# Units of the first conditioner in another order, and its shared expert in halves of 64 array columns

## The chip, the cores and the metric

The kernel runs on one core of a Trainium2 chip. A core has a matrix engine (PE, which loads weights as a separate step, PEld), a vector engine (DVE), a scalar engine for activations (ACT), a general engine (POOL), a sequencer for data movement (SP), and 16 DMA engines. Each engine runs its own instruction list; semaphores order them. The metric is the device time of one execution in microseconds (us), as the median of several runs.

## The reference

The input is x (32 batches of 128 positions of 128 numbers) and a condition vector for each batch. There are two layers. Each adds to x what a gated network computes from a conditioned x. In the first layer the conditioner is a small mixture of experts, and only it is touched here:

```python
topk_w, topk_i = jax.lax.top_k(gate_scores, 2)          # 2 of 4 experts for each batch
w_be = jnp.sum(topk_w[..., None] * onehot, axis=1)      # after normalising topk_w
for e in range(4):
    y = gelu(context_c @ ew1[e] + eb1[e]) @ ew2[e] + eb2[e]
    out = out + w_be[:, e][:, None, None] * mask[e][None, :, None] * y
shared = gelu(context_c @ sw1 + sb1) @ sw2 + sb2
return out + shared
```

The hidden width is 512. The mask drops 42 of the 128 positions for two of the experts. Then follow the first layer's gated network with 8 experts, computed densely, the second conditioner and the second feed-forward part.

## The kernel before, in words

Features lie on the 128 partitions. The 32 batches form 8 blocks of 4 batches, so a block is 128 partitions by 512 columns. All matrix products are in 32-bit floats; the profile shows each as two instructions.

The first conditioner has two kinds of work. The **shared expert** runs on all 8 blocks: `shared_up` (L255) makes four products of 512 columns into `us` (L260), each followed by an activation (L261); `shared_down` (L267) adds four products into `ys` (L271). Blocks 0 to 4 come first, blocks 5 to 7 (from `FIRST` on) after the routed units.

The **routed experts** run only for the chosen batches. Which expert gets which batch is known only on the chip: `schedule` (L331) ranks the batches of each expert and lays two batches of the same expert together as a pair. Thirty-two batches with two experts each give 64 slots. An expert with an odd number of batches leaves one batch over; it becomes a lone unit. There are at least 30 pairs (`LEAST`), pairs 30 and 31 may be missing, and so may each of the four lone units, numbered 32 to 35. For each unit:

- `fetch` (L434) loads the expert's weights (514.5 KB) on SP's queue, five units ahead (`NW` = 6 buffers). The expert's row is read from memory into SP's registers, four pairs at a time.
- `gather` (L451) copies the slots' inputs next to each other on DVE, two units ahead (`AHEAD`). The places are read into DVE's registers, four slots at a time.
- `unit_up` (L485) makes four products into `u` (L497) and four activations (L500); `unit_down` (L506) adds four products into `y` (L513) and DVE adds the gated result into `c0all` (L516, L520).

The width of a unit also depends on the data. `sized` (L468) tests a register on PE, ACT and DVE: the first arm (L472) is for pairs of unmasked experts (two times 128 columns), the other for masked ones (two times 86). For pair 30 and 31 the second arm holds one more test (L478), and each lone unit has its own (L482). In this run's data, by the operations counted in the trace, 16 pairs are 256 wide, 14 are 172 wide, two lone units are 128 and two 86 wide, and pairs 30 and 31 are missing.

`pipelined` (L200) writes the order: up of the next unit, then down of the present one. A planner in the language layer then orders each engine's instructions from this order and from modelled costs, so the traced order can differ: through most of the units here, a down step stands two units behind the up step. A conditional block stays whole. Small pieces of other work (gates, schedule, logits, transposes, folded weights) are put between the shared expert's products by the table `between` (L614).

`by_columns` (L231) makes one product as several, each with its own group of array columns: for n = 64, two products of 64 columns. The gated network uses it already (L236 for `g` and `u`), and its down products (L729) are also of 64 columns.

Of the kernel before, what the change touches and what calls it, by code (L numbers as in the profile page):

```python
# [39 lines left out]
P = 128  # L40
B, S, D = 32, 128, 128
# [7 lines left out]
NC = H // P  # L49
E0, EF, E1 = 4, 8, 8  # L50
# [5 lines left out]
NO_HEAD = (NHEAD, S)  # L56
# [9 lines left out]
NPAIR = B  # L66
LEAST = NPAIR - E0 // 2
# [32 lines left out]
def adaln_ffn(  # L100
# [3 lines left out]
    nc = tc.nc  # L104
# [9 lines left out]
    def mm_tile(name):  # L114
        return psum.tile([P, TB], F32, tag="mm", name=name, bufs=6)

    def y_tile(name):
        return psum.tile([P, TB], F32, tag="y", name=name, bufs=2)

    def const(shape, name, dtype=F32):  # L120
        return cpool.tile(shape, dtype, tag=name, name=name)
# [5 lines left out]
    sw1_t = wpool.tile([P, H], F32, tag="sw1", name="sw1_t")  # L127
    sw2_t = wpool.tile([P, NC, D], F32, tag="sw2", name="sw2_t")
# [7 lines left out]
    xT = [xall[:, b * TB : (b + 1) * TB] for b in range(NB)]  # L136
# [19 lines left out]
    for to, w in zip(downs_t, (s_w2, r_w2[: E1 // 2], r_w2[E1 // 2 :])):  # L156
        n = w.shape[0]
        nc.sync.dma_start(out=to.rearrange("p (e f) -> p e f", e=n), in_=w.rearrange("e d f -> d e f"))

    def col(name, i=0, n=1):  # L160
        return par[:, AT[name].start + i : AT[name].start + i + n]
# [53 lines left out]
    def sums(blk):  # L215
        xb = batches(xT[blk])
        at = slice(blk * BB, (blk + 1) * BB)
        lo = 0
        for to, n in ((head, NHEAD), (prop, NPROP), (wrist, NHEAD)):
            V.tensor_reduce(to[:, at], xb[:, :, lo : lo + n], AX.X, ALU.add)  # L220
            lo += n
# [5 lines left out]
    def before(*point):  # L227
        for do in between.pop(point, ()):
            do()

    def by_columns(ps, w, x, n):  # L231


        for at in range(0, P, n):
            own = slice(at, at + n)
            nc.tensor.matmul(ps[own, :], lhsT=w[:, own], rhs=x, start=True, stop=True)  # L236

# [13 lines left out]
    FIRST = NB - 3  # L253

    def shared_up(blk):  # L255
        h = work.tile([P, NC, TB], F32, tag="h", name=f"hs0_{blk}", bufs=3)
        ps = [mm_tile(f"us_{blk}_{c}") for c in range(NC)]
        for c in range(NC):
            before("up", "s", blk, c)
            nc.tensor.matmul(ps[c], lhsT=sw1_t[:, c * P : (c + 1) * P], rhs=xT[blk], start=True, stop=True)  # L260
            nc.scalar.activation(h[:, c, :], ps[c], AF.Gelu_apprx_tanh, bias=col("sb1", c))  # L261
        if blk < 2:
            for b in range(4 * blk, 4 * blk + 4):
                sums(b)
        return h

    def shared_down(blk, h):  # L267
        y = y_tile(f"ys_{blk}")
        for c in range(NC):
            before("down", "s", blk, c)  # L270
            nc.tensor.matmul(y, lhsT=sw2_t[:, c, :], rhs=h[:, c, :], start=(c == 0), stop=(c == NC - 1))  # L271
        if blk >= FIRST:
            V.scalar_tensor_tensor(c0T[blk], y, col("sb2"), c0T[blk], ALU.add, ALU.add)
        else:
            V.tensor_scalar(c0T[blk], y, col("sb2"), None, ALU.add)
# [49 lines left out]
    batch_at = const([1, NSLOT], "batch_at", I32)  # L325
    expert_at = const([1, NPAIR], "expert_at", I32)
# [65 lines left out]
    def spread_slots():  # L392
        ps = mm_tile("slots_ps")
        n = slot_sums.shape[-1]
        nc.tensor.matmul(ps[:, :n], lhsT=ones, rhs=slot_sums, start=True, stop=True)
        V.tensor_copy(batch_at, ps[:1, NSLOT : 2 * NSLOT])
        V.tensor_copy(expert_at, ps[:1, 2 * NSLOT : 2 * NSLOT + NPAIR])

        V.tensor_scalar(numbers, ps[:1, 2 * NSLOT + NPAIR : n], 1.0 / B, None, ALU.mult)
        V.tensor_copy(gate_of, ps[:, :NSLOT])  # L400
        E = mybir.EngineType
        engines = (E.PE, E.Activation, E.DVE)
        batch["full"], batch["pairs"], *batch["alone"] = registers(numbers, 0, engines, NPAIR, 2 + E0)
        for q in range(NW - 1):
            fetch(q)
        for q in range(AHEAD):
            gather(q)

    tl = const([P, B, E1], "tl")
# [13 lines left out]
    def registers(of, i, engines, top, n=4):  # L423
        return nc.values_load_multi_w_load_instructions(
            of[:, i : i + n], engines=engines, min_val=0, max_val=top,
            skip_runtime_bounds_check_because="sums of 0/1 times constants, within bounds by construction",
        )[1]

    weights, slots, batch = {}, {}, {}


    NUNIT = NPAIR + E0

    def fetch(q):  # L434


        i = q % NW
        if i < 4:
            w = wpool.tile([P, NPCOLS], F32, tag=f"w{i}", name=f"w_{q}")
        else:  # L440
            w = work.tile([P, NPCOLS], F32, tag="bsum", name=f"w_{q}", bufs=2)
        if q < NPAIR:
            if q % 4 == 0:
                batch["e"] = registers(expert_at, q, [mybir.EngineType.SP], (E0 - 1) * P)
            of = bass.ds(batch["e"][q % 4], P)
        else:
            of = slice((q - NPAIR) * P, (q - NPAIR + 1) * P)
        nc.sync.dma_start(out=w, in_=experts[of, :])
        weights[q] = w

    def gather(q):  # L451

        first = 2 * q if q < NPAIR else NPAIR + q
        if first % 4 == 0:
            batch["at"] = registers(batch_at, first, [mybir.EngineType.DVE], (B - 1) * S + NO_HEAD[0])
        batch[q] = batch["at"][first % 4 :][: slots_of(q)]
        x = work.tile([P, 2, S], F32, tag="bc", name=f"x_{q}", bufs=4)
        for i, at in enumerate(batch[q]):
            V.tensor_copy(x[:, i, :], xall[:, bass.ds(at, S)])
        slots[q] = x  # L460

    def slots_of(q):
        return 2 if q < NPAIR else 1

    NW = 6
    AHEAD = 2

    def sized(q, step):  # L468


        if q < NPAIR:
            with tc.If(batch["full"] > q) as cond:  # L472
                step(2, S)
            with cond.Else():
                if q < LEAST:
                    step(2, NSEEN)
                else:
                    with tc.If(batch["pairs"] > q):  # L478
                        step(2, NSEEN)
        else:  # L480
            e = q - NPAIR
            with tc.If(batch["alone"][e] > 0):  # L482
                step(1, S if e < NFULL else NSEEN)

    def unit_up(q):  # L485
        if q + NW - 1 < NUNIT:
            fetch(q + NW - 1)
        if q + AHEAD < NUNIT:
            gather(q + AHEAD)
        w, x = weights[q], slots.pop(q)  # L490
        h = work.tile([P, NC, 2, S], F32, tag="h", name=f"h0_{q}", bufs=3)
        ps = [mm_tile(f"u_{q}_{c}")[:, : 2 * S].rearrange("p (s t) -> p s t", s=2) for c in range(NC)]

        def step(m, n):
            for c in range(NC):
                w1 = w[:, ATP["w1"]][:, c * P : (c + 1) * P]
                nc.tensor.matmul(ps[c][:, :m, :n], lhsT=w1, rhs=x[:, :m, :n], start=True, stop=True)  # L497
            for c in range(NC):
                bias = w[:, ATP["eb1"]][:, c : c + 1]
                nc.scalar.activation(h[:, c, :m, :n], ps[c][:, :m, :n], AF.Gelu_apprx_tanh, bias=bias)  # L500

        sized(q, step)
        return h
# [122 lines left out]
    nc.gpsimd.memset(c0all[:, FIRST * TB :], 0.0)  # L626
    nc.gpsimd.memset(xall[:, NB * TB :], 0.0)
    L0 = {"s": (shared_up, shared_down), "p": (unit_up, unit_down)}
    units = [("s", b) for b in range(FIRST)] + [("p", q) for q in range(NUNIT)]
    units += [("s", b) for b in range(FIRST, NB)]  # L630
    pipelined(units, lambda k, i: L0[k][0](i), lambda k, i, h: L0[k][1](i, h))

# [213 lines left out]
    def sh_up(sb, k):  # L846
        e, c = divmod(k, 2)
        h = work.tile([P, SB, TB], F32, tag="h", name=f"hs_{sb}_{k}", bufs=3)
        for j in range(SB):
            x = x1T[SB * sb + j]  # L850
            g, u = mm_tile(f"g1_{sb}_{k}_{j}"), mm_tile(f"u1_{sb}_{k}_{j}")
            by_columns(g, sws_t[0][:, e, c, :], x, 32)
            by_columns(u, sws_t[1][:, e, c, :], x, 32)
            glu(g, u, h[:, j, :], f"s1_{sb}_{k}_{j}")
        return h
# [61 lines left out]
    units = [("s", sb, k) for sb in range(NS) for k in range(4)]  # L917
# [26 lines left out]
    def unit_down(kind, *at):  # L944
        STAGES[kind][1](*at)

    pipelined(units, unit_up, unit_down, after)
    low_out(1)

# [78 lines left out]
```

## Time and profile before

| what | value |
|---|---|
| median of 3 runs | 978.38 us (978.09 to 978.49) |
| profiled execution | 979.06 us, span 977.3 us |
| granted PE clock | 0.998 |
| PE busy | 962.9 us (99%) |
| DVE, ACT, POOL busy | 630.5, 345.0, 142.2 us |
| shared blocks 0 to 4, with gates and schedule | 4.9 to 46.4 us |
| routed units | 42.1 to 142.8 us |
| shared blocks 5 to 7, with logits and gates | 142.8 to 167.9 us |
| gated network and the rest | 167.9 us to the end |

In the profile, a row names the line, engine and operation, the output and inputs by the program's names, the shape, and how many. `128*64` before a shape means 128 array rows and 64 columns. Rows in order of time give the start, then the length of the merged group. A matmul's record ends with a modelled tail, so groups overlap on paper; the distance between two starts is the time that the first really takes. A bracket tells how long the engine stood idle before, and who is thought to have ended it.

### The profile page before, as it was taken

The page shows a single profiled execution, that of the slowest core. Times are in us where ns is not written, and L with a number is a line of the kernel's source. Part 1 is how long each engine was busy: PE and PEld are TensorE (multiplying, and loading weights), DVE is VectorE, ACT ScalarE, POOL GpSimd, SP SyncE. Part 2 cuts the span into 40 slices and gives each one's busy share as a digit, 9 for nine tenths or more (in the row PEclk, how much of TensorE's full clock was granted, in tenths as well). Part 3 has the DMA queues.
Part 4 walks back from the last instruction along what each step waited for, and adds up shares of the span by engine and source line. Part 5 has one row for each costly group of instructions (what it writes and reads, how often), then busy time and mean ns, then how long its engine had stood idle before and what let it go on. Part 6 is the DMA issues. An engine that isn't in the chain of part 4 may idle for free.

```text
span 977.3 us, 15574 instructions
## 1 busy us (share of the span) xinstructions
PE 962.9 (99%) x5998; PEld 450.8 (46%) x5998; DVE 630.5 (65%) x1130; ACT 345.0 (35%) x615; POOL 142.2 (15%) x151
## 2 busy tenths in 40 slices
PE   7999999999999999999999999999999999999997
PEld 3588974444444444444444444444444443323342
DVE  3444565666866776686676786567667656648593
ACT  5455544223322322232232332222223224335764
POOL 1000001100101011110101011010100001009680
PEclk9999999999999999999999999999999999999999
DMA  9745650000000000000000000000000000000002
GB/s 319 234 132 153 211 182 26 2 1 4 2 1 1 1 1 1 1 2 1 1 2 1 1 2 3 1 1 1 1 1 2 1 3 2 1 7 1 2 1 87
DMA packets 19043, 34.05 MB, mean 35 GB/s; under 512 B 1729, under 2 KB 9921, under 8 KB 18945
## 3 DMA queue, kind: packets, MB, share of 16 engines
q1 hardware_dynamic: 18096, 31.43, 10.3%
q10 hardware_dynamic: 864, 1.52, 0.4%
q8 instruction: 52, 0.85, 0.4%
q14 instruction: 31, 0.25, 0.1%
HBM read 30.59 MB, written 2.36 MB: 34 GB/s over the span
## 4 chain that ended last, share of the span: by engine, by line
PE 84%; DVE 2%; DVEq 0%; issue 0%
PE u L236 25%; PE g L236 25%; PE ya L729 10%; PE yb L729 8%; PE ur L236 6%; PE p_ps L844 2%; PE ul L895 1%; PE us L260 1%; PE ys L271 1%; PE q_ps L844 1%; PE y L513 0%; PE u L497 0%; DVE hf L704 0%; PE fold_ps L247 0%; DVE t L705 0%; DVE t L706 0%
## 5 line engine op out<-in xcount | busy, mean ns | idle before, releaser
L642 ACT ACTIVATE sf<-g 128x512 f32<-128x512 f32 x256 | 152.7, 597 | 438.1 <-PE g L236 432.0
L643 DVE TENSOR_TENSOR hf<-sf,u 128x512 f32<-128x512 f32 x256 | 174.9, 686 | 185.7 <-PE u L236 184.7
L236 PE MATMUL g<-c0all,wg_t 128*64 128x512 f32 x1024 | 270.3, 593 | 0.0
L236 PE MATMUL u<-cg,wu_t 128*64 128x512 f32 x1024 | 270.1, 592 | 0.0
L637 POOL PARTITION_BROADCAST fg<-fgT x64 | 71.9, 1135 | 662.4 <-DVE cg L685 499.1
L236 PEld LDWEIGHTS u<-cg,wu_t 128*64 128x64 f32 x1024 | 75.7, 137 | 145.2 <-issue 124.4
L236 PEld LDWEIGHTS g<-c0all,wg_t 128*64 128x64 f32 x1024 | 75.7, 137 | 120.2 <-issue 108.2
L729 PE MATMUL ya<-t,wd_t 128*64 128x256 f32 x512 | 121.6, 379 | 0.1
L637 POOL PARTITION_BROADCAST rg<-grows x64 | 67.8, 1187 | 145.4 <-DVE hr L878 76.8
L878 DVE TENSOR_TENSOR hr<-ar,rg 128x512 f32<-128x512 f32 x64 | 60.7, 996 | 15.8 <-ACT ar L877 15.8
L729 PEld LDWEIGHTS ya<-t,wd_t 128*64 128x64 f32 x512 | 69.9, 137 | 0.7 <-DVE t L706 0.6
L500 ACT ACTIVATE h<-u,w 128x256 f32<-128x256 f32 (+3 forms) x136 | 50.3, 429 | 54.3 <-PE u L497 54.3
L729 PE MATMUL yb<-hf,a_sum 128*64 128x256 f32 x512 | 69.1, 379 | 0.0
L729 PE MATMUL ya<-t,a_sum 128*64 128x256 f32 x256 | 65.9, 379 | 0.0
L729 PE MATMUL ya<-hf,wd_t 128*64 128x256 f32 x256 | 65.8, 379 | 0.0
L704 DVE TENSOR_TENSOR hf<-hf 128x512 f32<-128x512 f32 x64 | 62.7, 979 | 2.1
L236 PE MATMUL ur<-xall,rw_t 128*32 128x512 f32 x512 | 58.4, 592 | 0.0
L729 PEld LDWEIGHTS ya<-hf,wd_t 128*64 128x64 f32 x256 | 34.9, 137 | 42.8 <-issue 31.9
L513 PE MATMUL y<-h,w 128*128 128x256 f32 (+3 forms) x272 | 53.1, 338 | 1.0 <-DVE t L516 1.0
L497 PE MATMUL u<-x,w 128*128 128x256 f32 (+3 forms) x272 | 53.0, 338 | 1.1 <-DVEq L478 1.1
L497 PEld LDWEIGHTS u<-x,w 128*128 128x128 f32 x272 | 45.3, 190 | 5.7 <-ACT h L500 1.3
L877 ACT ACTIVATE ar<-ur 128x512 f32<-128x512 f32 x64 | 37.9, 598 | 27.6 <-PE ur L236 27.3
(215 smaller groups left out, 961.4 us busy)
## 6 DMA issues: line engine op xcount, KB each, us to landing
w<-in_experts SPq DMA_DIRECT2D x36, 514.5 KB
xall<-in_x SPq DMA_DIRECT2D x8, 256.0 KB
wg_t<-in_w_gate SPq DMA_DIRECT2D x8, 256.0 KB
wu_t<-in_w_up SPq DMA_DIRECT2D x8, 256.0 KB
wd_t<-in_w_down SPq DMA_DIRECT2D x8, 256.0 KB
out<-fin SPq DMA_DIRECT2D x4, 256.0 KB
out<-fin ACTq DMA_DIRECT2D x4, 256.0 KB
downs<-in_r_w SPq DMA_DIRECT2D x2, 256.0 KB
```

The costliest lines, as they stand in the source:

```text
L236: nc.tensor.matmul(ps[own, :], lhsT=w[:, own], rhs=x, start=True, stop=True)
L497: nc.tensor.matmul(ps[c][:, :m, :n], lhsT=w1, rhs=x[:, :m, :n], start=True, stop=True)
L500: nc.scalar.activation(h[:, c, :m, :n], ps[c][:, :m, :n], AF.Gelu_apprx_tanh, bias=bias)
L513: nc.tensor.matmul(y[:, :m, :n], lhsT=w2, rhs=h[:, c, :m, :n], start=(c == 0), stop=(c == NC - 1))
L637: nc.gpsimd.partition_broadcast(bc, row)
L642: nc.scalar.activation(s, ps_gate, AF.Silu)
L643: V.tensor_tensor(h, s, ps_up, ALU.mult)
L704: V.tensor_tensor(b12, b12, b11, ALU.subtract)
L729: nc.tensor.matmul(y[half, n], lhsT=w[:, c, :], rhs=h[:, c, :], start=False, stop=(e == EF - 1 and last))
L844: nc.tensor.matmul(y[32 * j : 32 * (j + 1), :], lhsT=w, rhs=h[:, j, :], start=first, stop=last)
L877: nc.scalar.activation(a, ps, AF.Gelu)
L878: V.tensor_tensor(h[:, j, :], a, gate, ALU.mult)
```

## The change

Two parts. First, the units: a list `UNITS` holds pairs 0 to 29 in order, with the six units that may be missing (30 to 35) put in at even distances: 0-3, 30, 4-7, 31, 8-11, 32, 12-16, 33, 17-20, 34, 21-24, 35, 25-29. `fetch` now takes a place in this list; `gather` still takes a unit's number. SP's registers are still read for four pairs at a time for pairs below 30, and singly for pairs 30 and 31. DVE's registers are read for each unit by itself.

Second, the shared expert: the products at L260 and L271 go through `by_columns` with 64 columns, which now also takes the flags for the first and last product of a sum.

```diff
-    def by_columns(ps, w, x, n):
+    def by_columns(ps, w, x, n, first=True, last=True):
         for at in range(0, P, n):
             own = slice(at, at + n)
-            nc.tensor.matmul(ps[own, :], lhsT=w[:, own], rhs=x, start=True, stop=True)
+            nc.tensor.matmul(ps[own, :], lhsT=w[:, own], rhs=x, start=first, stop=last)
...
-            nc.tensor.matmul(ps[c], lhsT=sw1_t[:, c * P : (c + 1) * P], rhs=xT[blk], start=True, stop=True)
+            by_columns(ps[c], sw1_t[:, c * P : (c + 1) * P], xT[blk], D // 2)
...
-            nc.tensor.matmul(y, lhsT=sw2_t[:, c, :], rhs=h[:, c, :], start=(c == 0), stop=(c == NC - 1))
+            by_columns(y, sw2_t[:, c, :], h[:, c, :], D // 2, c == 0, c == NC - 1)
...
-        for q in range(NW - 1):
-            fetch(q)
-        for q in range(AHEAD):
+        for i in range(NW - 1):
+            fetch(i)
+        for q in UNITS[:AHEAD]:
             gather(q)
...
-    NUNIT = NPAIR + E0
+    UNITS = list(range(LEAST))
+    maybe = list(range(LEAST, NPAIR + E0))
+    for i in reversed(range(len(maybe))):
+        UNITS.insert((i + 1) * LEAST // (len(maybe) + 1), maybe[i])

-    def fetch(q):
-        i = q % NW
+    def fetch(i):
+        q = UNITS[i]
+        i %= NW
...
         if q < NPAIR:
-            if q % 4 == 0:
-                batch["e"] = registers(expert_at, q, [mybir.EngineType.SP], (E0 - 1) * P)
-            of = bass.ds(batch["e"][q % 4], P)
+            def found(n):
+                return registers(expert_at, q, [mybir.EngineType.SP], (E0 - 1) * P, n)
+            if q < LEAST and q % 4 == 0:
+                batch["e"] = found(min(4, LEAST - q))
+            of = bass.ds(batch["e"][q % 4] if q < LEAST else found(1)[0], P)
...
-        if first % 4 == 0:
-            batch["at"] = registers(batch_at, first, [mybir.EngineType.DVE], (B - 1) * S + NO_HEAD[0])
-        batch[q] = batch["at"][first % 4 :][: slots_of(q)]
+        batch[q] = registers(
+            batch_at, first, [mybir.EngineType.DVE], (B - 1) * S + NO_HEAD[0], slots_of(q)
+        )
...
     def unit_up(q):
-        if q + NW - 1 < NUNIT:
-            fetch(q + NW - 1)
-        if q + AHEAD < NUNIT:
-            gather(q + AHEAD)
+        i = UNITS.index(q)
+        if i + NW - 1 < len(UNITS):
+            fetch(i + NW - 1)
+        for ahead in UNITS[i + AHEAD : i + AHEAD + 1]:
+            gather(ahead)
...
-    units = [("s", b) for b in range(FIRST)] + [("p", q) for q in range(NUNIT)]
+    units = [("s", b) for b in range(FIRST)] + [("p", q) for q in UNITS]
```

## The prediction

> **What bounds the kernel now.** I read the page's busy times and its chain first, then the matrix engine (PE) in order of time over the last expert units of the first conditioner, then the branches there, then two places where PE changes its array form.
>
> ```profile
> PE 962.9 (99%) x5998; PEld 450.8 (46%) x5998; DVE 630.5 (65%) x1130; ACT 345.0 (35%) x615; POOL 142.2 (15%) x151
> PE 84%; DVE 2%; DVEq 0%; issue 0%
> ```
>
> PE sets the end: a change counts only by the PE stream time that it adds or the PE gaps that it opens or closes. The edited stage ends where L236 begins, at 167.94 us.
>
> PE in order of time (start, length with the modelled tail, operation, count); starts are subtracted below:
>
> ```profile
> 127.92 1.33 PE L497 MATMUL u<-x,w 128*128 128x172 f32 x8
> 129.08 1.33 PE L513 MATMUL y<-h,w 128*128 128x172 f32 x8
> 130.87 1.43 PE L513 MATMUL y<-h,w 128*128 128x172 f32 x8 [0.46 <-DVE t L516]
> 132.87 1.41 PE L513 MATMUL y<-h,w 128*128 128x172 f32 x8 [0.57 <-DVE t L516]
> 134.12 1.05 PE L497 MATMUL u<-x,w 128*128 128x128 f32 x8
> 136.26 1.13 PE L497 MATMUL u<-x,w 128*128 128x128 f32 x8 [1.10 <-DVEq L478]
> 137.23 1.95 PE L513 MATMUL y<-h,w 128*128 128x128 f32 x16
> 139.02 1.02 PE L497 MATMUL u<-x,w 128*128 128x86 f32 x8
> ...
> 142.78 1.06 PE L260 MATMUL us<-xall,sw_t 128*128 128x512 f32 x2
> ```
>
> A step of a 172-wide pair takes 129.08 - 127.92 = 1.16 us. After it stand gaps: 130.87 - 129.08 - 1.16 = 0.63; 132.87 - 130.87 - 1.16 = 0.84; 136.26 - 134.12 - 0.89 = 1.25. (0.89 is a step of a lone expert, half of 139.02 - 137.23; its eight instructions start 112 ns apart for 128 columns and for 86, so weight loads pace it.) Who ended them is named as DVE, but the branch row says more:
>
> ```profile
> L478 PEldq COMPARE_BRANCH  x4: 202/205/212, 128.0 to 135.6; - x4
> L478 PEldq EVENT_SEMAPHORE  x4: 51/51/51, 130.5 to 135.9; - x4
> ```
>
> Four times PE came to L478, the test for a pair that may be missing, and skipped the body: pairs 30 and 31 are missing here, up and down, and the four lone experts are all present (rows of 128 and 86 columns). A skip makes PE wait for its own last matmul (130.41 by its modelled end), bump its semaphore (130.45) and take another branch; the next load starts at 130.87. The stretch 129.08 to 142.78 is 13.70 us; its work is 3 x 1.16 + 8 x 0.89 = 10.6. Of the 3.1 us left, 0.63 + 0.84 + 1.25 = 2.7 stand at the four skips, the rest is restarts and short waits of lone units.
>
> **Part one, the moved units.** The order becomes 0-3, 30, 4-7, 31, 8-11, 32, 12-16, 33, 17-20, 34, 21-24, 35, 25-29. It moves the skips; it removes none. Each still drains PE, whoever stands next. One skip costs 0.63 to 0.84 by the rows (the two behind 134.12 share 1.25). What differs is the neighbour: pairs 30 and 31 now stand among the 16 pairs that take the first arm of L472, whose branch on PE is short where it is not taken:
>
> ```profile
> L472 PEldq COMPARE_BRANCH  x96: 65/176/340, 36.5 to 135.4; - x96
> ```
>
> 65 ns in place of some 205 takes 0.14 off. So 4 x (0.58 to 0.72), I take 4 x 0.65 = 2.6 against 2.7, and with no gain from the neighbour 4 x 0.74 = 2.9. The lone units' other waits, 3.1 - 2.7 = 0.4, of which about 0.1 belongs to restarts after skips: among pairs of 1.16 to 1.73 us a step nothing waits on their short ScalarE and VectorE steps. Part one: -0.1 - 0.3 = **-0.4 us** (from -0.8 to +0.1).
>
> What moves with the units. The fetches stay 36 of 514.5 KB on SP's queue; the two missing units' weights now pass ahead of pairs 4 and 8. Pair 4's goes out sixth instead of fifth, about 0.9 us later on SP (a register load and a DMA issue more), and lands up to 514.5 KB / 183 GB/s = 2.8 us later (that rate: the 10 us from 40 us on). Six times 514.5 KB at that rate and the 208 GB/s of 30 to 40 us are in by about 51 us, counted from SP's first fetch at 34.8; pair 4 is used at 56.75. Cover gone: up to 2.8 us. Two more SP register loads of 0.30 us stand before fetches that wait 1.8 us for a buffer anyway. On DVE, slot numbers are read for each unit, not for two: some 19 more register loads of 0.34 us and 0.08 after. Where such a load stands before the copies today (124.76 us), DVE still waits 0.66 us for PE's y; over the 172-wide pairs:
>
> ```profile
> 104.00:129.00 25.00, 25.00 (x174) 25.00 (x173) 14.46 (x55) 13.50 (x43) 0.00 (x0) 1.00 0.74 230
> ```
>
> PE is busy 25.00 of 25.00 us here, DVE 14.46, so the loads cost nothing; uncovered they would be 19 x 0.42 = 8 us at most, and nothing in the trace makes DVE that late. Behind a DVE load stand only its own copies for a unit two steps ahead. Weight traffic is at 0.74 of the DMA engines; a lone unit lasts 1.79 us, which asks 514.5 / 1.79 = 287 GB/s for that moment, below the 348 that the stretch from 10 to 20 us shows, with five units fetched ahead.
>
> **Part two, the halves.** PE after that stage, and a place in the gated network where one 128-column transpose stands between 64-column work:
>
> ```profile
> 160.98 7.03 PE L271 MATMUL ys<-hs,sw_t 128*128 128x512 f32 x16
> 167.94 1.08 PE L236 MATMUL g<-c0all,wg_t 128*64 128x512 f32 x4
> 168.85 1.03 PE L236 MATMUL u<-cg,wu_t 128*64 128x512 f32 x4
> ...
> 236.74 0.59 PE L729 MATMUL yb<-hf,wd_t 128*64 128x256 f32 x2
> 237.27 0.33 PE L558 MATMUL fg_ps<-ident,cwT 128*128 128x128 f32 x1
> 237.53 1.08 PE L236 MATMUL g<-c0all,wg_t 128*64 128x512 f32 x4
> 238.43 1.03 PE L236 MATMUL u<-cg,wu_t 128*64 128x512 f32 x4
> ```
>
> A product of 128 columns is two instructions at 0.429, 0.858 us. In halves it is four, two running side by side, and g and u also start 0.86 apart (L236 in steady flow). So 64 products become 128 pairs of halves at no stream time; the 128 further matmuls and loads hide under the streams as L236's do.
>
> What it adds is changes of array form. ys to g: 7.03 is 6.96 by starts, against 16 x 0.429 = 6.866, +0.09; g 0.91 against 0.86, +0.05; so 128 to 64 is **0.145**. The lone transpose: 237.27 - 236.74 = 0.53 against 2 x 0.216, +0.10; 0.26 against 0.11 for the same transpose among 128-column work (160.87 to 160.98), +0.15; g +0.05: a round trip is **0.30**, so 64 to 128 is 0.155. Now count:
> - start: shared block 3 to pair 0, to shared block 4, to pair 1 (42.09, 43.81, 46.39 today): 0.155 + 0.145 + 0.155 = +0.455
> - last pair to shared block 5: +0.145, less 0.04 that its first interval loses today: +0.10
> - round trips for the transposes L544 and L558: +0.60; for L247, 0.30 less 0.085 that ys already loses after it (155.63 to 157.44 is 1.80, four intervals are 1.716): +0.22
> - ys to g is now 64 to 64: -0.145
> - five returns from 32-column or 32-row work (gate, order, slots, times, logits): today +0.105 (149.06 to 150.88 is 1.82 against 1.716), to 64 columns +0.05: -0.27
>
> Sum **+0.96 us**. A rule speaks for more: the Trainium skill, "TensorEngine Tiling (Array Packing)", Tiling Modes, says that changing the tiling mode drains the engine. A full drain would show the tail past the stream (an L236 matmul lasts 0.592, its stream 0.429: 0.163) and then a 64-column load (0.137), 0.30 a change. The list has nine more changes net: 2.7 us. The two rows show half of that, so I take the rows and keep 2.7 as the upper end; the lower is 0.5, if the planner groups work of one form.
>
> **Sum.** +0.96 - 0.4 = +0.55. The profiled execution took 979.06 (span 977.3 and 1.76 around it): 979.6 for one like it. It lay 0.7 above the median of the runs, 978.38, so the median goes to **978.9 us**, +0.06%. The bound for a change that this kernel's measurement can tell is 0.2%, 1.96 us.
>
> **Rivals.**
> - *The planner mixes forms at the seam* (slower). The last units are now real pairs with 1.16 us steps beside shared blocks 5 and 6, and the written order alternates them. If single 64-column products are dealt between the 128-column steps there and about pair 0, each round trip is +0.30. It passes 0.2% from 1.4 / 0.30, five more round trips; six give 978.9 + 1.8 = 980.7, which is also what the drain rule gives. For it: g, u and ya are already dealt singly in the gated network. Against: today the stage keeps shared blocks whole (42.09 to 46.39).
> - *A skip in mid-stream costs more than in the tail* (slower). PE jumps over two bodies and finds the code behind them not there, or the weights of pair 4 late: 2.8 us, 981.7. Against: 96 branches at L472 with 340 ns at most, and the 6 us of cover above.
> - *The scattering hides the skips too* (faster). All 3.1 us go in place of 0.4: 978.38 - 3.1 + 0.96 = 976.2. For it: the gaps are put down to other engines in the PE rows. Against: the wait is PE's on itself, and no neighbour's work can run in it.
> - *The halves change nothing*: switches are free for these shapes, only part one stays: 978.0. Against: both rows above.
>
> **How the numbers follow.** Near-cancelling, 977.9 to 979.9: 0.57. Mixed forms or full drains: 0.17, a third of it below the bound. Mid-stream stall: 0.09. Skips hidden: 0.07. Halves free: 0.10. So faster 0.07, same 0.57 + 0.10 + 0.06 = 0.73, slower 0.20. Leaving out the skips hidden below and the far end above gives 977.0 to 981.2.
>
> **What would show it.** Skips: four L478 semaphore waits on PE, now between about 55 and 85 us, each with a gap of 0.5 to 0.8; none from 129 us on. Halves: L260 and L271 no longer as 128x512 at 128 columns; product starts 0.86 apart; the rows that follow a 128-column step longer by 0.05, those before it by 0.1. The gated network should start 0.3 to 0.8 us later than 167.94 and the rest keep its length. Wrong it would be if PE waits for weights or for x between 55 and 130 us, if the gap at a skip is over 1 us, or if the planner's order of the later stages shifts, whose last 20 us have PE gaps that I haven't counted.

## The result, and the profile after

| | before | changed |
|---|---|---|
| median of 6 runs each | 978.16 us (977.59 to 978.49) | 983.76 us (982.80 to 984.05) |
| ratio | | 1.0052, 95% interval 1.0040 to 1.0064 |
| profiled execution | 979.06 us, span 977.3 | 983.98 us, span 982.2 |
| granted PE clock in it | 0.998 | 0.998 |

The change costs 5.6 us by the medians, 3.9 to 6.3 by the interval. The prediction was 978.9 with a range to 981.2, so it was wrong. In the changed kernel the up and down products of the units are L506 and L522, the shared expert's products are all L236, the test for a missing pair is L486, and L529, L544, L247 and L558 have become L538, L553, L247 and L567.

The page's busy times and chain, changed kernel:

```profile
PE 968.4 (99%) x6126; PEld 444.1 (45%) x6126; DVE 631.3 (64%) x1130; ACT 344.4 (35%) x615; POOL 142.0 (14%) x151
PE 90%; DVE 2%; issue 0%; DVEq 0%
```

PE still sets the end, and it is busy 5.5 us longer. So nearly all of the time went into PE's own stream, not into waits for another engine. PE in order of time, changed kernel, where the shared expert meets the first pairs (`x2` is one half: a 32-bit product shows as two instructions):

```profile
36.95 3.65 PE L236 MATMUL ys<-hs,sw_t 128*64 128x512 f32 x14
40.53 1.99 PE L506 MATMUL u<-x,w 128*128 128x256 f32 x8
42.45 2.80 PE L236 MATMUL ys<-hs,sw_t 128*64 128x512 f32 x12
45.18 1.99 PE L506 MATMUL u<-x,w 128*128 128x256 f32 x8
47.10 1.07 PE L236 MATMUL ys<-hs,sw_t 128*64 128x512 f32 x2
48.10 1.99 PE L522 MATMUL y<-h,w 128*128 128x256 f32 x8
49.94 1.89 PE L506 MATMUL u<-x,w 128*128 128x256 f32 x8
```

The planner treats a half as an instruction like any other. It laid seven halves ahead of pair 0, six between pair 0 and pair 1, and **one alone** behind pair 1. Block 4's eight halves are split here into one (among the seven ahead of pair 0), six and one; the profile does not tell which half is which. Halves of different products can run side by side too, as a `ys` half and a `g` half do below. A half alone does not run in half the time of its product: from 47.10 to 48.10 is 1.00 us, which is the 0.86 of a whole product and 0.14 for changes of form on both sides. Two halves side by side take 0.86 together. So each run with an odd number of halves costs 0.43 more, and there are two here (7 and 1).

The same view of the seam between the last pairs and shared block 5, and what follows:

```profile
140.24 1.07 PE L236 MATMUL us<-xall,sw_t 128*64 128x512 f32 x2
141.25 1.43 PE L522 MATMUL y<-h,w 128*128 128x172 f32 x8
142.61 1.94 PE L236 MATMUL us<-xall,sw_t 128*64 128x512 f32 x8
144.48 1.43 PE L522 MATMUL y<-h,w 128*128 128x172 f32 x8
...
153.15 0.66 PE L553 MATMUL lg_b<-ident,lgT 128*128 128x128 f32 x4
153.74 1.07 PE L236 MATMUL ys<-hs,sw_t 128*64 128x512 f32 x2
154.74 2.87 PE L247 MATMUL fold_ps<-par,downs 128*128 128x32 f32 x24
157.53 3.17 PE L236 MATMUL ys<-hs,sw_t 128*64 128x512 f32 x8
160.48 4.12 PE L236 MATMUL us<-xall,sw_t 128*64 128x512 f32 x16
164.43 1.02 PE L236 MATMUL ys<-hs,sw_t 128*64 128x512 f32 x2
165.38 0.33 PE L567 MATMUL fg_ps<-ident,cwT 128*128 128x128 f32 x1
165.64 6.65 PE L236 MATMUL ys<-hs,sw_t 128*64 128x512 f32 x29
171.71 0.59 PE L236 MATMUL g<-c0all,wg_t 128*64 128x512 f32 x1
172.13 0.59 PE L236 MATMUL ys<-hs,sw_t 128*64 128x512 f32 x1
...
174.18 1.08 PE L236 MATMUL u<-cg,wu_t 128*64 128x512 f32 x4 [0.17 <-DVE cg L694]
```

Halves are dealt between the 172-wide steps (1.36 us each here, 1.17 among their like), one stands between transposes and folding products, and the runs between changes are odd four times: 1 at 140.24, 1 at 153.74, 13 from 157.53 on, and the 15 `ys` halves from 165.64 on. The last of these 15 shares its time with a half of `g` (171.71 and 172.13), which has the same form, so PE's own stream loses nothing there. But the first `u` waits, by way of DVE, for the last `ys`: from its second instruction at 172.13 to `u` are 2.05 us here, and 2.09 in the moved order alone. So the 0.43 by which that `ys` is late counts there too. The row at 157.53 shows something else: its four halves take 2.95 to the next row's start at 160.48, and 1.77 in other profiles of the same kernel. Its cause is in the clock. Windows of 5 us of the same profile, with PE's busy time first and the granted clock third from the end:

```profile
155.00:160.00 5.00, 5.00 (x32) 3.33 (x33) 1.09 (x4) 0.67 (x2) 0.00 (x0) 0.81 0.00 0
160.00:165.00 5.00, 5.00 (x20) 1.47 (x16) 3.23 (x9) 2.87 (x4) 0.00 (x0) 0.85 0.00 0
```

PE is busy throughout, but for 3.41 us from 158.10 on it was given half its clock, which cost 1.7 us.

To sum the parts for all kernels I cut each trace at three starts: the first `ys` product, unit 2's first `u` product, and the first gated unit's last four `yb` products (184.75 us before). The differences of these starts, in us:

| kernel | first product to first ys | ys to unit 2 | unit 2 to last yb | placed by the middle two, against before | ratio to before (95%), from the timed runs |
|---|---|---|---|---|---|
| before | 9.77 | 35.17 | 134.91 | | |
| changed, first profile | 8.48 | 36.73 | 139.76 | +6.41, of it 1.7 the clock | 1.0052 (1.0040 to 1.0064) |
| changed, three more profiles | 9.40, 9.61, 9.37 | 36.73 | 137.96, 138.08, 137.96 | +4.6 to +4.7 | 1.0058 (1.0044 to 1.0071), five runs beside the first of the three |
| moved order alone | 8.80 | 35.17 | 134.75 | -0.16 | 1.0000 (0.9992 to 1.0008) |
| halves alone | 9.50 | 36.73 | 135.70 | +2.35 | 1.0039 (1.0026 to 1.0053) |
| block 4 down whole | 8.54 | 35.19 | 138.05 | +3.16 | 1.0033 (1.0021 to 1.0045) |
| folding products moved | 9.19 | 36.73 | 138.41 | +5.06 | 1.0053 (1.0039 to 1.0066) |
| halves kept together | 9.39 | 35.19 | 135.67 | +0.78 | 1.0009 (1.0001 to 1.0017) |
| halves in blocks 0 to 2 | 9.34 | 35.28 | 134.79 | -0.01 | 1.0000 (0.9991 to 1.0008) |
| missing pairs left out | 9.56 | 35.17 | 132.12 | -2.78 | 0.9973 (0.9964 to 0.9983) |
| one block per pair | 8.43 | 35.17 | 134.24 | -0.67 | 0.9995 (0.9988 to 1.0001) |
| one block for both pairs | 9.66 | 35.17 | 133.67 | -1.24 | 0.9986 (0.9980 to 0.9993) |

From the last `yb` to the kernel's last four products (`o_ps`) it is 785.5 to 785.6 us in every one of them. The first column differs from execution to execution with the start of the clock, not with the change (last section). The changed kernel's cost is thus 1.56 at the start and 3.05 to 3.17 behind it, 4.6 to 4.7 us, which lies in both of its intervals. The medians stand 5.6 and 5.9 us above. A stretch at half clock in some executions is a part of what lies between (below), and the first column may be another; the rest is not placed. For the halves alone the placed 2.35 us is just under its interval (2.5 to 5.2 us).

### The profile page after: what moved, and what is told of

It reads as the page before. It is cut to its first block, busy times and chain, and to the rows that moved or that the text cites. A ratio compares the mean times of both kernels' runs of the same rounds, so it can differ in the third digit from the quotient of the medians.

```text
span 982.2 us, 15841 instructions
## 1 busy us (share of the span) xinstructions
PE 968.4 (99%) x6126; PEld 444.1 (45%) x6126; DVE 631.3 (64%) x1130; ACT 344.4 (35%) x615; POOL 142.0 (14%) x151
## 4 chain that ended last, share of the span: by engine, by line
PE 90%; DVE 2%; issue 0%; DVEq 0%
PE u L236 25%; PE g L236 25%; PE ya L738 10%; PE yb L738 8%; PE ur L236 6%; PE y L522 4%; PE u L506 3%; PE p_ps L853 2%; PE ys L236 1%; PE us L236 1%; PE ul L904 1%; PE q_ps L853 1%; PE fold_ps L247 0%; DVE hf L713 0%; DVE t L714 0%; DVE t L715 0%
## 5 line engine op out<-in xcount | busy, mean ns | idle before, releaser
L236 PE MATMUL g<-c0all,wg_t 128*64 128x512 f32 x1024 | 271.1, 592 | 0.0
L236 PE MATMUL u<-cg,wu_t 128*64 128x512 f32 x1024 | 270.1, 592 | 0.2 <-DVE cg L694 0.2
L236 PEld LDWEIGHTS u<-cg,wu_t 128*64 128x64 f32 x1024 | 75.6, 137 | 145.2 <-issue 124.1
L236 PEld LDWEIGHTS g<-c0all,wg_t 128*64 128x64 f32 x1024 | 76.1, 137 | 120.0 <-issue 109.1
L236 PE MATMUL ur<-xall,rw_t 128*32 128x512 f32 x512 | 58.4, 592 | 0.0
L522 PE MATMUL y<-h,w 128*128 128x256 f32 (+3 forms) x272 | 53.0, 340 | 1.0 <-PEq L486 1.0
L506 PE MATMUL u<-x,w 128*128 128x256 f32 (+3 forms) x272 | 52.9, 339 | 0.4 <-PEq L486 0.4
L522 PEld LDWEIGHTS y<-h,w 128*128 128x128 f32 x272 | 44.4, 190 | 7.7 <-DVE c0all L529 3.0
```

Source lines behind the costliest of these rows:

```text
L236: nc.tensor.matmul(ps[own, :], lhsT=w[:, own], rhs=x, start=first, stop=last)
L522: nc.tensor.matmul(y[:, :m, :n], lhsT=w2, rhs=h[:, c, :m, :n], start=(c == 0), stop=(c == NC - 1))
```

## The experiments

Theory A: the halves cost the time, by standing alone (0.43 each) and by more changes of form. Rival B: the moved units cost it, by late weights or skips in mid-stream. Theory C: the stretch at half clock follows the thin work in front of it, that is transposes and folding products of few columns.

**Each part alone.** `order_only` has the list of units, with whole products (edits are against the changed kernel where nothing else is said):

```diff
-            by_columns(ps[c], sw1_t[:, c * P : (c + 1) * P], xT[blk], D // 2)
+            nc.tensor.matmul(ps[c], lhsT=sw1_t[:, c * P : (c + 1) * P], rhs=xT[blk], start=True, stop=True)
...
-            by_columns(y, sw2_t[:, c, :], h[:, c, :], D // 2, c == 0, c == NC - 1)
+            nc.tensor.matmul(y, lhsT=sw2_t[:, c, :], rhs=h[:, c, :], start=(c == 0), stop=(c == NC - 1))
```

> Part one alone: the units that may be missing stand among the pairs, the shared expert's products stay whole (128 columns). Theory A (the time is lost by halves that run alone, by changes between forms of 64 and 128 columns, and by a stretch at half clock, all of them part two's): 977.4 to 978.2 us, that is 0 to 0.8 below the kernel before; no stretch at half clock between 20 and 200 us; the units take 92.3 to 92.7 us from unit 2's first product to the last unit's down product, against 92.94 before. Rival B (the moved units cost the time, by late weights or skips in mid-stream): 982 us or more, and gaps above 1 us in front of the pairs behind a skip.

`halves_only` is the kernel before with the two lines the other way round, and the flags in `by_columns`.

> Part two alone: the units in the order of the kernel before, the shared expert's products in halves. Its tail has every half beside its partner, its start has the same two lone halves as the changed kernel. Theory A: start +1.5 (two lone halves at 0.43, some five changes of form at 0.15), tail +0.7 to +1.0 (changes of form alone), no stretch at half clock in the tail: 979.2 to 980.7 us. Theory A without the lone halves (changes of form alone): 978.9. Rival B: 978.2, as before.

Measured: 978.60 us (13 runs) for the moved order and 981.38 us (5 runs) for the halves, against 978.60 of the kernel before beside them. Both lie above what was expected, by 0.4 and 0.7 us; the halves' 2.8 us rests on five runs, and its trace places 2.35. B falls: the moved order costs nothing, and no step ahead of a skip takes more than 0.6 us beyond its stream. It shows no gain in time either. From unit 2 to its tail's start (the first `us` behind the units) it takes 90.21, and two down steps of 1.17 stand behind, 92.55 against 92.94: this is the -0.4 that was expected. But the gain does not reach the end. VectorE in order of time where the gated network begins, in the kernel before and then in the moved order alone (`cg` are the gated rows that the first `u` there needs):

```profile
167.16 1.04 DVE L685 TENSOR_TENSOR cg<-c0all,fg 128x512 f32<-128x512 f32 x1 [1.79 <-POOL fg L637]
168.12 0.74 DVE L273 SCALAR_TENSOR_TENSOR c0all<-ys,par,c0all 128x512 f32<-128x512 f32 x1
```

```profile
166.72 0.75 DVE L273 SCALAR_TENSOR_TENSOR c0all<-ys,par,c0all 128x512 f32<-128x512 f32 x1 [2.68 <-PE ys L271]
167.39 1.81 DVE L694 TENSOR_TENSOR cg<-c0all,fg 128x512 f32<-128x512 f32 x2
```

Before, `cg` came ahead of the last addition of the shared expert, as soon as POOL had spread the gates. In the moved order the planner put it behind that addition, which waits for PE's last `ys`, though POOL begins to spread the gates at 166.18 and takes some 0.8 us. So the first `u` comes 1.57 us after the first `g`, against 0.91 before; 0.38 of this are, by difference, zeroing products that were further back in the order, and 0.28 is lost. With -0.44 up to the first `g` that makes the -0.16 of the table. The changed kernel has the same order on DVE. This is read from the rows; no run changed that order alone.

The halves alone have the same start as the changed kernel (36.73) but only +0.79 behind it, where the changed kernel has 3.05 to 3.17. In the old order a run of lone units stands before shared block 5, no halves get between them, and no run is odd in the tail. So 2.4 to 2.5 us of the changed kernel's cost come from the two parts **together**.

**Block 4's down products whole.**

```diff
-            by_columns(y, sw2_t[:, c, :], h[:, c, :], D // 2, c == 0, c == NC - 1)
+            by_columns(y, sw2_t[:, c, :], h[:, c, :], D if blk == FIRST - 1 else D // 2, c == 0, c == NC - 1)
```

> The changed kernel, with the down products of shared block 4 alone whole again: they are the ones that stand split around the first pairs' blocks. Theory A: two lone halves less at 0.43 and four changes of form less at 0.15 to 0.20, so 1.4 to 1.6 below the changed kernel, 982.2 us, with the stretch at half clock near 158 us still there. If lone halves cost nothing and only changes of form do: 0.6 to 0.8 below. Rival B: no difference.

Measured: 981.32 us (6 runs). PE in order of time, at the place of the first fence above:

```profile
40.84 1.89 PE L506 MATMUL u<-x,w 128*128 128x256 f32 x8
42.57 2.74 PE L236 MATMUL ys<-hs,sw_t 128*128 128x512 f32 x6
45.14 1.89 PE L506 MATMUL u<-x,w 128*128 128x256 f32 x8
```

The 256-wide steps are back at 1.73 (42.57 - 40.84) from 1.92, and the stretch to unit 2 falls from 36.73 to 35.19, by 1.54: the two lone halves (0.86) and, by difference, four changes of form (0.68, 0.17 each). That leaves 0.02 over the kernel before, although four shared blocks still run in halves. The medians differ by more (2.4 us from the changed kernel), and the half-clock stretch, which was expected to stay, is absent.

**The folding products elsewhere.**

```diff
-        ("down", "s", FIRST, 2): [fold_down],
+        ("up", "s", FIRST + 2, 2): [fold_down],
```

> The changed kernel with the folding products (N = 32) behind two up products of the last block, so that no thin work stands in a row after the logits' transposes; as many lone halves as in the changed kernel. Theory C (the half-clock stretch at 158 us follows the row of thin work: transposes, one lone half, 12 products of 32 columns): no stretch at half clock between 20 and 200 us, and 1.3 to 1.8 below the changed kernel, 982.1 us. If the stretch has another cause or is chance, it comes as often as in the changed kernel and the time stays at 983.8.

Measured: 983.70 us (5 runs), as the changed kernel. There is no half-clock stretch in its profile, and the time is where it was: theory C's 982.1 did not come. The stretch is not part of the changed kernel's usual time, as its further profiles show below, and the tail itself is 0.4 longer here.

**Halves kept together.** Those products whose halves stood apart are whole, ten of 64. So 54 remain in halves, not the 26 that the expectation names.

```diff
+    UP_WHOLE = {(FIRST, c) for c in range(NC)}
+    DOWN_WHOLE = {(FIRST - 1, c) for c in range(NC)} | {(FIRST, 1), (FIRST + 1, 0)}
...
-            by_columns(ps[c], sw1_t[:, c * P : (c + 1) * P], xT[blk], D // 2)
+            by_columns(ps[c], sw1_t[:, c * P : (c + 1) * P], xT[blk], D if (blk, c) in UP_WHOLE else D // 2)
...
-            by_columns(y, sw2_t[:, c, :], h[:, c, :], D // 2, c == 0, c == NC - 1)
+            by_columns(y, sw2_t[:, c, :], h[:, c, :], D if (blk, c) in DOWN_WHOLE else D // 2, c == 0, c == NC - 1)
```

> The changed kernel with those products whole whose halves stood apart: the down products of block 4, the up products of block 5, one down product each of blocks 5 and 6. The other 26 products of the 32 of a whole... stay in halves, every half beside its partner. Theory A (a half whose partner stands behind another form costs a pass of its own, 0.43): against the kernel with block 4 whole alone (981.3) four lone halves less, 1.7, and some five changes of form less, 0.7: 978.8 to 979.4 us; from the start of the shared expert's tail to the second gated unit 44.7 to 45.5 us, against 49.45 in the changed kernel. If halves cost by themselves, wherever they stand: 980.5 or more.

Measured: 979.29 us (13 runs). PE in order of time, its seam:

```profile
139.60 1.02 PE L236 MATMUL us<-xall,sw_t 128*128 128x512 f32 x2
140.45 1.33 PE L524 MATMUL y<-h,w 128*128 128x172 f32 x8
141.62 2.74 PE L236 MATMUL us<-xall,sw_t 128*128 128x512 f32 x6
144.19 1.33 PE L524 MATMUL y<-h,w 128*128 128x172 f32 x8
```

The same steps stand between at the seam, but the pieces are whole products of 0.86, and the pair's steps take 1.17 again. From the seam's first product to the last `yb` it is 45.36 us, where the changed kernel's undisturbed profiles have 47.74: 2.38 less, of which four lone halves are 1.72 and the rest, 0.66, is by difference some five changes of form. With 54 of 64 products in halves the kernel is within 0.8 us of the moved order alone. It is not the halves that cost, but the halves apart.

**Halves where nothing stands between.**

```diff
-            by_columns(ps[c], sw1_t[:, c * P : (c + 1) * P], xT[blk], D // 2)
+            if blk < 3:
+                by_columns(ps[c], sw1_t[:, c * P : (c + 1) * P], xT[blk], D // 2)
+            else:
+                nc.tensor.matmul(ps[c], lhsT=sw1_t[:, c * P : (c + 1) * P], rhs=xT[blk], start=True, stop=True)
```

and the same for the down products.

> The changed kernel's order, with halves in the shared blocks 0 to 2 alone, where nothing stands between them. Theory A: halves side by side cost what a whole product costs: the time of the moved order alone, 978.6 us (978.2 to 979.0), and 35.1 to 35.3 us from the first down product to unit 2. If halves make the start of the kernel shorter or longer by themselves (first product to first down product 8.5 us in the changed kernel, 9.8 in the one before), this stretch is within 0.3 us of 8.5; if that stretch is chance it lies anywhere from 8.4 to 9.9.

Measured: 978.19 us (13 runs), no clear difference from the kernel before (978.46 beside it): halves side by side cost nothing, and they gain nothing. The stretch to unit 2 is 35.28, +0.11. The first stretch is 9.34, not 8.5: it is not the halves that shortened it.

**What a skip costs.** This and the next are built on the moved order with whole products. `no_absent` leaves pairs 30 and 31, which are missing in this data, out of the list:

```diff
-    maybe = list(range(LEAST, NPAIR + E0))
+    maybe = list(range(NPAIR, NPAIR + E0))
```

> The moved order with whole products, and the two pairs that are missing in this data (30 and 31) left out of the list altogether, so that the kernel no longer handles data in which they are there. Theory: each of the four places at which a missing unit is passed over costs 0.5 to 0.7 us: 2.0 to 2.6 below the moved order alone, 976.0 to 976.6 us, unless the gates' chain (logits to the first product with gated rows, 19.7 us in both orders) holds the end, which would leave the gain whole too, since the chain starts earlier by as much. If a skip is hidden: 978.6.

`one_skip` keeps them, with up and down in one conditional block:

```diff
+        if LEAST <= q < NPAIR:
+            return h, step
         sized(q, step)
-        return h
+        return h, None
...
         def step(m, n):
+            if up_step is not None:
+                up_step(m, n)
```

> The moved order with whole products; the two pairs that may be missing do their up and their down products in one conditional block, so that a missing one is passed over once instead of twice. Theory: half of what four skips cost: 1.0 to 1.3 below the moved order alone, 977.3 to 977.6 us. If one skip costs as much as two in a row of a unit (the wait is for the unit's weights, not for the branch): 978.6.

Measured: 975.71 (10 runs) and 977.98 us (21 runs), the first 0.3 below what was expected, the second 0.4 above. Four skips cost 134.75 - 132.12 = 2.63 in the traces of the moved order without and with this edit, 0.66 each. The skips of the changed kernel, first by line, then the pair behind one in order of time:

```profile
L486 PEldq COMPARE_BRANCH  x4: 208/214/218, 52.0 to 74.7; - x4
L486 PEldq EVENT_SEMAPHORE  x4: 51/51/51, 55.3 to 78.0; - x4
```

```profile
53.39 1.89 PE L506 MATMUL u<-x,w 128*128 128x256 f32 x8
55.69 1.99 PE L522 MATMUL y<-h,w 128*128 128x256 f32 x8 [0.41 <-PEq L486]
57.51 1.89 PE L506 MATMUL u<-x,w 128*128 128x256 f32 x8
```

The step ahead takes 2.30 instead of 1.73, +0.57, and the one behind 1.82, +0.09. One block per pair should have halved this, and did not: two down steps now follow each other, and the second starts late by a wait for DVE, so one skip costs 0.91 (16 instructions 4.36 apart in start, 3.45 without a skip). Of 1.3 expected, 0.68 came between the units and 0.51 was left at the last `yb`; the rest is a longer wait ahead of the first `u` with gated rows.

**One block for both pairs.** This is the version that the runs point to: whole products, the moved order, pairs 30 and 31 next to each other, and one test around both. It holds the edit of `one_skip` too; the `False` tells `sized` to leave out pair 30's own test.

```diff
+    UNITS.remove(NPAIR - 1)
+    UNITS.insert(UNITS.index(LEAST) + 1, NPAIR - 1)
...
+        if q == LEAST:
+            pending.append(step)
+        elif up_step is not None:
+            with tc.If(batch["pairs"] > LEAST):
+                sized(LEAST, pending.pop(), False)
+                sized(q, step)
+        else:
+            sized(q, step)
```

> The moved order with whole products; the two pairs that may be missing stand next to each other, and both do their up and down products in one conditional block, so that the data of this case passes over one block where the changed kernel passes over four. Theory: the four skips cost 2.6 to 2.7 together and one block costs 0.9, as each of the two in the kernel with one block per pair: 1.7 below the moved order alone, 976.6 to 977.0 us, less some 0.1 to 0.2 if the gates' chain holds the start of the gated network. Rival (what is left is not the skips): 978.

Measured: 976.93 us (21 runs) against 978.06, ratio 0.9986 (0.9980 to 0.9993): the lowest ratio among the kernels that keep the code for every case, below the kernel before and the changed one. Of the 1.6 that the units gain over the moved order alone, 0.5 goes back to the wait ahead of the first gated `u`: its first `cg` starts at 166.68, as POOL has spread the gates (165.85 and 0.8 us), 0.81 behind the start of the last addition, where it follows by 0.67 in the moved order alone. So here the gates' own chain is, by a little, the last to come. What such a block costs on data in which these pairs are there was not measured.

**The changed kernel again**, unedited:

> The changed kernel once more, unedited. Theory C (the stretch at half clock near 158 us follows the thin work in front of it): it is there again, and from the start of the shared expert's tail to the second gated unit takes 49.4 us. If that stretch is chance: it is absent or elsewhere, this part takes 47.7 to 47.8 us as it did with block 4 whole, and the kernel stands 4.6 to 5.0 us above the kernel before (lone halves and changes of form 1.56 at the start and 3.15 behind it).

> The changed kernel unedited, for a third profile. The parts that the traces place give 4.6 us over the kernel before, its medians 5.6 and 5.9; a stretch at half clock (1.7 us) in half of the executions would be the rest. If the thin work near 155 us tends to bring the stretch: half clock between 156 and 166 us in at least one of this and the next profile, and 49.4 us from the tail's start to the second gated unit there. If the one stretch seen was chance: neither has one in that place, and both take 47.7 us.

> The changed kernel unedited, for a fourth profile; expected as for the third.

Measured: 983.98 us (5 runs) in the first, single runs of 983.53 and 983.16 us in the others. The first stands 5.9 us above the kernel before, more than the 4.6 to 5.0 expected. None of the three has the stretch at half clock. The window of the last that answers to the first of those above:

```profile
155.00:160.00 5.00, 5.00 (x34) 3.38 (x34) 1.67 (x6) 1.49 (x2) 0.00 (x0) 1.00 0.00 0
```

So the stretch stood in one of four profiles of the same kernel, though the thin work was there in all four. Theory C is not shown. It is not excluded either: the clock changes at borders 3.413 us apart (last section), and in the three profiles without the stretch such a border falls among the folding products (156.88, 157.07 and 156.56), in the one with it none does.

How often the stretch comes can be judged from the mean granted clock, which was taken in every run. No profile without the stretch has a mean under 0.9975. A mean of 0.996 or 0.997 stands at 6 of the 42 runs of kernels with halves behind the units (changed 2 of 13, halves alone 1 of 5, folding products moved 1 of 5, halves kept together 2 of 13, block 4 whole 0 of 6) and at none of the 168 runs of kernels with whole products there. The changed kernel's first profile, at 0.9975, is one more. So the halves behind the units seem to bring such a stretch in about one run of six, with the folding products moved too; what in them does it stays open. At 1.7 us in 3 of 13 runs it adds 0.4 us to the changed kernel's mean.

## Why the prediction was wrong

**What bounds the kernel**: right. PE's stream is nearly all that counted, and no weight, slot or register load was late. The six units' moved fetches and some 19 more register loads on DVE cost nothing that the traces show.

**Part one**, -0.4: right in its size between the units (92.55 against 92.94), and four skips at 4 x 0.65 = 2.6 measured 2.63. How the -0.4 divides into 0.1 for the skips' neighbours and 0.3 for the lone units was not measured. What it did not count, though it named a shifted order of the later stages as a sign of being wrong, is the planner's new order on DVE at the gated network's start, which takes 0.28 back; the whole is -0.16 in the traces, inside its range of -0.8 to +0.1.

**Part two**, +0.96: this failed. The step is "So 64 products become 128 pairs of halves at no stream time". It holds for halves side by side: four such products of the changed kernel's first `ys` take 3.43 us to the next start, and blocks 0 to 2 in halves cost 0.1 us at most. But it supposes that two halves stay together, and nothing in the code binds them. Six odd runs of halves, two at the start and four in the tail, cost 6 x 0.43 = 2.6 us, where this step had 0. The prediction named the planner only for its changes of form, not for this.

**The count of changes of form** failed too, in the number and less in the price: 2.2 us with what else is left in the changed kernel, where it had 0.96. Where nothing is dealt between, it held: the tail of the halves alone is 0.79 longer, and the count's terms for the tail make some 0.7. The rival of mixed forms at the seam was described as it came, "single 64-column products are dealt between the 128-column steps there and about pair 0", and was held less likely since the kernel before keeps shared blocks whole at pair 0. That argument was taken from 42.09 to 46.39 us, where six instructions stand together; it overlooked that block 4's four products were already split there, one ahead of pair 0 and three behind. In the moved order the last units are pairs, whose steps leave room for single products: the moved order alone with whole products deals them in the same places. The prices were near. Of each change a part stands ahead of the first row in the new form and a part in that row's first interval. From 128 to 64 columns these are 0.309 in place of 0.216 and 0.480 in place of 0.429, 0.145 together, as counted (42.14 to 42.93). The other way they are 0.522 in place of 0.429 and 0.320 in place of 0.216 (40.01 to 40.85), 0.20 together for a step of 256 columns, where 0.155 was counted.

**The rule that was weighed**, the Trainium skill's "TensorEngine Tiling (Array Packing)", Tiling Modes: the rows stand. A round trip costs 0.34, not twice the 0.30 that was estimated for a full drain. Its upper end of 2.7 us would still have been nearer to the time, for another reason than the one it was given for.

**The sum** with the terms as measured: part one -0.16 in the place of -0.4; at the start +1.56 (two lone halves 0.86, changes of form 0.7) in the place of some +0.2; behind it 3.2 over the moved order alone (four lone halves 1.72, changes of form and what is left 1.5) in the place of some +0.7. Together 4.6.

## What to carry to other kernels

- Where one product is cut into column groups that are to run side by side, the pair is the unit of account: look where a planner may put other work between its parts, and count each group that it leaves alone at the price of the whole product. Cut only those products that have no other form for a neighbour, and ask what the cut is to gain: here it gained nothing even there (978.19 against 978.46, no clear difference).
- Two edits can cost more together than the sum of each alone. Here the moved order brought steps with room for single products next to work that had just become divisible.
- A moved step changes the planner's order on the other engines too. Look at what the next stage's first operand stands behind in its engine's list.

## What the runs showed of the hardware

**The start depends on the clock's window.** The stretch of the first eight products (16 instructions) lies between 8.43 and 9.77 us in these traces. PE starts at half clock (its first passes start 0.85 us apart, later ones 0.43), and the records of the granted clock begin at full clock between 7.86 and 10.57 us: 2.97 to 5.68 us after the first product. The stretch is 6.87 (16 x 0.429) plus half of that time in each: 6.87 + 5.68 / 2 = 9.71 for 9.77 before, 6.87 + 3.19 / 2 = 8.46 for 8.48 in the changed kernel. From then on every change of the granted clock lies at a whole number of 3.413 us, the fall behind the last products too (after 282 to 285 of them): in the changed kernel's first profile the half-clock stretch begins 150.19 us later, 44 x 3.413, and lasts 3.41. The Trainium skill's "TensorE: Matmul & The Clock Gate", Part 1, tells of a free-running window of this length and of a varying number of slow products at the start, which these traces agree with; it gives the transition's variation as ±500 ns, and here it is 2.7 us from the earliest to the latest, worth 1.3 us of the time. Between the fastest and the slowest run of the kernel before lie 2.4 us (977.49 to 979.85); this may be 1.3 of them.

**A busy PE can lose its clock.** The same part has the clock fall after an idle window. Here PE's records show it busy for all of 5.00 us about the place, though short gaps could hide behind the modelled ends. The window ahead of the fall, 154.68 to 158.10, holds the 24 folding instructions of 32 columns and the first two halves behind them. In two other kernels' traces, both with whole products (missing pairs left out, one block for both pairs), the folding products also lie within one window and the clock stays, so they alone are not the condition. What the window counts was not settled.

**A lone half of the array takes a product's full time**, 0.86 us by starts for 512 columns of 32-bit floats: 1.00 from 47.10 to 48.10 with the changes of form, and 0.86 for two side by side.
